# Causal attention scores accumulated across key tiles from differences of keys, in a two-layer transformer kernel

## The chip, the cores and the metric

The kernel runs on one core of one Trainium2 chip. The metric is the device time of one execution in microseconds, smaller is better. Times of before come from three runs; the profile is one more execution of the same program, recorded by the hardware profiler.

Engines in the profile: PE is TensorE's matmul, PEld its loads of stationary operands (they overlap PE), DVE is VectorE, ACT is ScalarE, POOL is GpSimd, SP issues nearly all DMAs. Matmuls write to PSUM, which has eight banks of 128 x 512 float32.

## What is computed

Two transformer layers over one sequence of S = 4096 rows of E = 256 features with 16 heads of 16. `x` is [1, 4096, 256].

```python
xn = _layernorm(x)
x = x + _L0_attn_ref(xn, ...) + _L0_ffn_ref(xn, ...)   # pass a=0: sparse attention; an fp8 product
xn = _layernorm(x)
x = x + _L1_attn_ref(xn, ...) + _L1_ffn_ref(xn, ...)   # a=1; and a block that holds a=2

# a=0: each block of 128 queries sees its own 128 keys and every 8th key, causal by an added -10000
# a=1: causal attention over all keys, queries and keys rotated (RoPE)
scores = jnp.einsum('bhqd,bhkd->bhqk', Q, K) / math.sqrt(Dh)
scores = jnp.where(causal, scores, jnp.finfo(scores.dtype).min)
attn = jax.nn.softmax(scores, axis=-1)
y = jnp.einsum('bhqk,bhkd->bhqd', attn, V)
# a=2, in _L1_ffn_ref: the same causal attention, with RMS-normalised q and k per head,
# then a mixture of four experts, two chosen for each row
```

## The kernel before

**Tiling.** Queries are worked in 8 chunks (`NCH`) of 512 (`CW`), keys in tiles of 128 (`TPC` = 4 to a chunk), heads in 4 groups (`G`) of 4 (`HPG`). A *unit* is one pass `a`, one group and one chunk of queries; there are 32 units of each pass. A causal unit of chunk `ch` (a = 1 or 2) has 4(ch + 1) key tiles, the last four of them in the queries' own chunk, where the part above the diagonal is masked. A unit of a=0 has four tiles of strided keys and one local one.

**Operands.** Each head's queries and keys are split into a rounded high part and the rest, and laid out as 64 rows a head, so that one product over 64 rows of PE gives an accurate score. `split_stored` does this for a finished half of the heads (ACT copy, POOL subtraction, two SP stores) and puts the rows into DRAM scratch `q_d` and `k_d`; `load_rows` brings them back for a unit, with tags `q`, `km` (keys for the maxima) and `ke` (keys for the exponentials). PE runs two heads at a time, one in its upper and one in its lower 64 rows: `p` in 0, 1 is the pair of heads, `j` the half. `emit` interleaves the two halves' instruction streams by their cost.

**Two passes over the keys.** First the maxima: `causal_max` multiplies a tile of 128 queries with 512 keys into two banks (`pm`), and DVE reduces each bank to one column of `mx`. Half 1's bank is reduced first, then half 0's. When all of a unit's maxima are there, `reduced`, `shift` and `shifted` turn the negated maxima into rows (`rows`, in the profile's names), in high and low parts. Then the exponentials: `causal_exp` multiplies a tile of 128 keys with the 512 queries into a bank `st`, adds the shift by a second product of a constant `pick` with `rows` (in the profile `st_a<-rows,pick_r`), adds the mask on the own chunk (`st_a<-mcol_sb,identb_sb`), and ACT writes exp(st) to `pt`. `values` multiplies the four heads' `pt` with the values (eight matmuls a key tile in the profile) and accumulates over key tiles in one bank `po`.

**PSUM.** Three rings of banks: `max` with 3 (maxima), `bank` with 4 (scores, and every other product: projections, experts), `acc` with 1 (`po`). A pair of maxima takes two banks of `max`, a pair of scores two of `bank`.

**What sets the order.** Every engine issues in the order in which the program emits (`InOrder`, line 53; so all rows of the profile show L53). The order comes from `Schedule`, a heap of pieces by a key (planned place, in units of a chunk's length) that is emptied at the end. A piece may take banks of a ring (`add_ring`), or be a *fill* that opens a bank and has a *drain* with a due time (`add_open`); `run` emits opened drains early when a ring has no room left. `unit` gives the keys: exponentials of key tile kt and pair p at a0 + 0.25 kt + 0.125 p + 0.06, values of kt 0.45 after a0 + 0.25 kt. So the order on PE in the middle of a unit is: scores of pair 0, of pair 1, values of the tile before, and so on. A unit's maxima run some units ahead (`lag`); each call of `exponentials` takes one waiting pair of maxima along as its `side`, so that a maxima product of one half runs beside a scores product of the other:

```python
own = [make(st[j], j, half_rows(j)) for j in range(2)]
emit(own[0] + side[0], side[1] + own[1])
```

The output projection of a pass and chunk (`projected`, two fills `pp` with drains `added`) comes 1.5 to 1.7 chunk lengths after the last group's unit has ended, beside the exponentials of a later unit.

**Between chunks.** For chunks 1 to 6 a section with its own place in the plan (`between`) runs the experts of chunk ch − 1, the preparation of chunk ch + 1 for a = 1 and 2 (`prepare1`: projections, rotation or norm, `split_stored`) and of chunk ch + 3 for a = 0 (`prepare0`). The first 620 us or so prepare the first chunks beside the a=0 units (`spread`).

Of the kernel before, what the change touches and what calls it, by code (L numbers as in the profile page):

```python
# [21 lines left out]
H = 16  # L22
# [43 lines left out]
class Schedule:  # L66
# [9 lines left out]
    def __init__(self):  # L76
        self.items, self.n = [], 0
        self.opened = {ring: [] for ring in self.RINGS}

    def _push(self, key, *item):  # L80
# [3 lines left out]
    def add(self, key, fn, *args):  # L84
        self._push(key, None, 0, lambda: fn(*args), None)

    def add_ring(self, key, ring, banks, fn, *args):
        self._push(key, ring, banks, lambda: fn(*args), None)

# [3 lines left out]
    def run(self):  # L93
        opened = self.opened
        while self.items or any(opened.values()):
            due, ring0 = min(((min(due for due, _ in o), r) for r, o in opened.items() if o), default=(None, None))
            if not self.items or (due is not None and due <= self.items[0][0]):
                opened[ring0].pop(0)[1]()
                continue
            _, _, (ring, banks, fn, drain) = heapq.heappop(self.items)  # L100
            if ring is not None:
                while len(opened[ring]) + banks > self.RINGS[ring]:
                    opened[ring].pop(0)[1]()
            fn()
            if drain is not None:
                opened[ring].append(drain)
# [3 lines left out]
def tile_two_layers(ctx: ExitStack, tc, d, out):  # L110
# [24 lines left out]

    def bank_tile(name, ring="bank"):
        return ps[ring].tile([P, CW], F32, tag=ring, name=name)
# [12 lines left out]
    q_d = [dram.tile([H * 4 * D, S], F32, name=f"q_d{a}") for a in range(3)]  # L150
    k_d = [dram.tile([H * 4 * D, S + (CW if a == 0 else 0)], F32, name=f"k_d{a}") for a in range(3)]
    v_d = [dram.tile([G, NCH + 1, P, TPC * VW], F32, name=f"v_d{a}") for a in range(3)]

# [9 lines left out]
    with ExitStack() as at:  # L163
# [181 lines left out]
        def split_stored(s, dst, half, col, what, name):  # L345

            hl = halves(name)
            split(s, hl)
            stored(dst, hl, half, col, what)

        def normalised(todo, x, nm, eng=None):
# [163 lines left out]
        def prepare1(ch):  # L515
# [35 lines left out]
            for n, (what, dst) in enumerate((("k", k_d[1]), ("q", q_d[1]))):  # L551
# [26 lines left out]
                for half in range(2):  # L578
# [4 lines left out]
                        ),  # L583
                    )

            act_piece(todo, weighted)
# [3 lines left out]
            for what, n, wcol, dst in (("k", 3, 1, k_d[2]), ("q", 4, 0, q_d[2])):  # L590
# [57 lines left out]
                for half in range(2):  # L648
                    act_piece(stores, lambda half=half, f=st2: f(half))
                rest.append((products, norms2, mul2, turns, stores))  # L650

# [240 lines left out]
        def load_k(u, kc, tag):  # L892
            u[tag, kc] = load_rows(u, k_d, kc * CW, tag, 3)

# [15 lines left out]
        def tt(t):  # L910
            return slice(t * P, (t + 1) * P)

        def product(dst, lhs, rhs, start=False, stop=False):

            return max(P, int(np.prod(dst.shape[1:]))), lambda: pe.matmul(dst, lhs, rhs, start=start, stop=stop)

        def own_mask(dst, eye, mask, r, blocks=0, short=0):


            got = []  # L920
            for i in (1 - short, short):
# [4 lines left out]
                if blocks:  # L926
                    m = m.unsqueeze(1).to_broadcast([64, blocks, m.shape[1]])
                got.append(product(to, eye[r, i], m, i != short and bool(blocks), i == short and not blocks))
            return got

        class Maxima:
# [10 lines left out]
            def __call__(self):  # L942
                if not self.done:
                    emit(*self.begin())
                    self.reduce()
# [110 lines left out]
        def exponentials(u, kt, p, lo, make, key):  # L1056

            mx = next_maxima(key)
            side = mx.begin() if mx else ([], [])
            st = [bank_tile(f"st_{u['nm']}_{kt}_{2 * p + j}") for j in range(2)]  # L1060
            own = [make(st[j], j, half_rows(j)) for j in range(2)]
# [8 lines left out]
        def causal_exp(u, kt, p, key):  # L1070
            kc, t = divmod(kt, TPC)
            own = kc == u["ch"]
            lo = t * P if own else 0

            def make(st, j, r):
                seq = [
                    product(st[:, lo:], u["ke", kc][p][r, tt(t)], u["q"][p][r, lo:], True),
                    product(st[:, lo:], pick[r, 0, p, :], u["sh"][r, lo:], stop=not own),
                ]
                return seq + (own_mask(st[:, lo : lo + P], identb, mcol, r) if own else [])  # L1080

            exponentials(u, kt, p, lo, make, key)
# [136 lines left out]

        sched = Schedule()  # L1220

        def put(key, fn, ring=None, drain=None, delay=0.11):
# [12 lines left out]
        def unit(a, g, ch, a0, lag, m0, own_at):  # L1235
# [21 lines left out]
            for i, make in enumerate(makes):  # L1257
                key = m0 + size * (i + 0.5) / len(makes)
                maxima.append((key, len(maxima), Maxima(make)))
                sched.add_ring(key, "max", 2, maxima[-1][2])  # L1260
            r0 = a0 - min(lag - size, 1.0)
# [5 lines left out]
            for kt in range(int(4 * size)):  # L1267
                for p in range(2):
                    key = a0 + 0.25 * kt + 0.125 * p + 0.06
                    if a:  # L1270
                        sched.add_ring(key, "bank", 2, causal_exp, u, kt, p, key)
                    elif kt < 4:
                        sched.add_ring(key, "bank", 2, strided_exp, u, kt, p, key)
                    else:
                        sched.add_ring(key, "bank", 2, local_exp, u, p, key)
                key = a0 + 0.25 * kt + 0.45
# [283 lines left out]
```

## Time and profile before

| | |
|---|---|
| three runs, median (lowest to highest) | 4963.56 us (4957.01 to 4964.4) |
| span of the profiled execution | 4961.8 us |
| its mean granted PE clock | 0.982 |
| PE, PEld busy | 4779.2 us, 2517.8 us |
| DVE, ACT, POOL busy | 3665.9 us, 3075.4 us, 886.2 us |
| products of the shift (`st_a<-rows,pick_r`) | 5248, busy 1749.6 us |
| exponentials on ACT (`pt_a<-st_a`) | 5248, busy 2590.3 us |
| plain maxima on DVE (`mx_a<-pm_a`) | 3584, busy 2220.8 us |
| DMA | 732.87 MB, queue q1 44.3% of 16 engines' span |

The profiled execution has no other time of its own than its span; the median of the runs lies 1.8 us above it. Rows of groups read "line engine op out<-in xcount | busy us, mean ns of one | idle us before them, and what ended most of it"; `64*128 64x512` is a stationary tile of 64 rows by 128 and a moving one of 64 by 512. In the timeline each row is start in us, duration in us, engine and operation; instructions of the same kind that follow closely are drawn together with their count (x4), and the bracket holds the idle time ahead of them and what ended it. In a row of windows the columns are the stretch, its length, busy us of PE, PEld, DVE, ACT and POOL with counts, the granted clock, the share of the DMA engines, and GB/s.

### The profile page before, as it was taken

Reading aid. Unit: us, or ns where it says so; the run is one execution under the profiler, and the core shown is the slowest. Engines: PE = TensorE matmul, PEld = TensorE weight load, DVE = VectorE, ACT = ScalarE, POOL = GpSimd, SP = SyncE. Lnnn points to the kernel's source line nnn. Section 1 sums busy time; section 2 is a strip of 40 time slices with the busy share of each in tenths; the row PEclk is TensorE's granted clock in tenths of the full one; section 3 lists DMA queues with packets and bytes.
Section 4 is the critical chain, followed back from the end, with each engine's and each line's share of the span. In section 5 each row is a group of like instructions: output and inputs, shape, how many; then the busy total and the mean of one; then the engine's idle time right before and its main releaser. Section 6 shows DMA issues by size and latency. Waiting matters only on the chain.

```text
span 4961.8 us, 95104 instructions
## 1 busy us (share of the span) xinstructions
PE 4779.2 (96%) x34528; PEld 2517.8 (51%) x34528; DVE 3665.9 (74%) x8399; ACT 3075.4 (62%) x6193; POOL 886.2 (18%) x1541
## 2 busy tenths in 40 slices
PE   6888899999999999999999999999999999999999
PEld 3455555555554555544545445544445544444445
DVE  4776783895689749896598984798984898989701
ACT  2555463675567547775477774677773777777752
POOL 2544423213110221103101002001002000000000
PEclk8999899999999999999999999999999999999999
DMA  6656555545544454444544334443333433333322
GB/s 205 210 157 220 188 172 167 194 152 185 175 156 138 151 191 135 147 133 153 188 129 148 129 129 129 163 135 132 125 133 110 164 131 121 124 108 128 97 81 77
DMA packets 480302, 732.87 MB, mean 148 GB/s; under 512 B 84052, under 2 KB 185940, under 8 KB 479832
## 3 DMA queue, kind: packets, MB, share of 16 engines
q1 hardware_dynamic: 477232, 725.40, 44.3%
q8 instruction: 273, 4.47, 0.4%
q10 hardware_dynamic: 2600, 1.39, 0.1%
q14 instruction: 197, 1.61, 0.1%
HBM read 582.71 MB, written 143.95 MB: 146 GB/s over the span
## 4 chain that ended last, share of the span: by engine, by line
PE 54%; DVE 6%; issue 4%; POOL 1%; ACT 0%; DMA 0%; SPq 0%; POOLq 0%; ACTq 0%; DVEq 0%
PE st_a L53 19%; PE po_a L53 16%; PE pm_a L53 8%; DVE mx_a L53 5%; PE pe_m L53 2%; PE pp L53 1%; PE pv L53 1%; PE ph_m3l L53 1%; PE ph_m2l L53 1%; PE ph_m4l L53 1%; PE ph_m5l L53 1%; PE pq L53 1%; PE ph_m7l L53 1%; PE pk L53 1%; DVE pms_a L53 0%
## 5 line engine op out<-in xcount | busy, mean ns | idle before, releaser
L53 ACT ACTIVATE pt_a<-st_a 128x512 f32<-128x512 f32 (+3 forms) x5248 | 2590.3, 574 | 1066.8 <-PE st_a L53 1003.5
L53 DVE TENSOR_REDUCE mx_a<-pm_a 128x1 f32<-128x512 f32 x3584 | 2220.8, 682 | 316.8 <-PE pm_a L53 218.8
L53 PE MATMUL pm_a<-km_a,q_a 64*128 64x512 f32 (+3 forms) x4608 | 1798.6, 434 | 50.0 <-DVE mx_a L53 45.2
L53 PE MATMUL st_a<-q_a,ke_a 64*128 64x512 f32 (+3 forms) x5632 | 1765.9, 397 | 5.4 <-ACT pt_a L53 1.8
L53 PE MATMUL st_a<-rows,pick_r 64*128 64x512 f32 (+3 forms) x5248 | 1749.6, 400 | 0.0
L53 PEld LDWEIGHTS st_a<-q_a,ke_a 64*128 64x128 f32 x5632 | 902.9, 187 | 1009.6 <-ACT pt_a L53 931.9
L53 PE MATMUL po_a<-pt_a,v 128*32 128x512 f32 (+3 forms) x11264 | 1327.4, 550 | 0.0
L53 PEld LDWEIGHTS pm_a<-km_a,q_a 64*128 64x128 f32 x4608 | 837.2, 185 | 417.3 <-DVE mx_a L53 339.7
L53 PEld LDWEIGHTS st_a<-rows,pick_r 64*128 64x128 f32 x5248 | 949.6, 186 | 56.2 <-issue 0.4
L53 DVE CUSTOM_DVE_ANT_0 pm_a<-pm_a,never_sb 128x512 f32<-128x512 f32 (+3 forms) x1024 | 477.6, 517 | 233.3 <-PE pm_a L53 195.7
L53 DVE CUSTOM_DVE_ANT_0 pms_a<-pms_a,hidden_sb 128x512 f32<-128x512 f32 x512 | 338.0, 721 | 71.2 <-PE pms_a L53 60.9
L53 PEld LDWEIGHTS po_a<-pt_a,v 128*32 128x32 f32 x11264 | 228.3, 108 | 293.8 <-issue 256.5
L53 POOL CAST pad<-nm_a 128x16 fp32r<-128x16 f32 x96 | 21.1, 219 | 1902.6 <-DVE nm_a L53 1902.6
L53 PE MATMUL pms_a<-km_a,q_a 64*128 64x512 f32 x512 | 221.7, 491 | 59.9 <-DVE mx_a L53 44.7
L53 POOL CAST rows<-tu_a 8x128 fp32r<-8x128 f32 x768 | 226.4, 295 | 214.4 <-DVE tu_a L53 119.1
L53 DVE SCALAR_TENSOR_TENSOR acc_m<-pe_m,g_wt_m,acc_m 128x192 f32<-128x192 f32 x128 | 53.2, 417 | 246.3 <-PE pe_m L53 243.1
L53 PE MATMUL st_a<-mcol_sb,identb_sb 64*128 64x128 bf16 (+1 forms) x2048 | 233.2, 209 | 0.0
L53 DVE DVE_READ_ACCUMULATOR2_ANT mx_a<- 128x1 f32 x1536 | 216.9, 141 | 0.0
L53 POOL TENSOR_TENSOR om_a<-od_a,rd_a 128x256 f32<-128x256 f32 x96 | 64.6, 673 | 675.7 <-DVE rd_a L53 651.8
L53 PEld LDWEIGHTS pms_a<-km_a,q_a 64*128 64x128 f32 x512 | 96.7, 192 | 99.8 <-DVE mx_a L53 80.1
L53 PEld LDWEIGHTS <-identb_sb 64*128 64x128 bf16 x2048 | 114.6, 96 | 9.1 <-issue 1.5
L53 POOL TENSOR_TENSOR xa<-xa,pa 128x512 f32<-128x512 f32 (+1 forms) x48 | 56.9, 1184 | 237.3 <-issue 118.8
(406 smaller groups left out, 3942.2 us busy)
## 6 DMA issues: line engine op xcount, KB each, us to landing
km_a<-k_d SPq DMA_DIRECT2D x352, 512.0 KB, 4.8
ke_a<-k_d SPq DMA_DIRECT2D x352, 512.0 KB, 3.9
k_d<-hl_k SPq DMA_DIRECT2D x100, 512.0 KB, 3.9
q_d<-hl_q SPq DMA_DIRECT2D x96, 512.0 KB, 4.7
q_a<-q_d SPq DMA_DIRECT2D x96, 512.0 KB, 5.1
v<-v_d SPq DMA_DIRECT2D x352, 136.0 KB, 4.8
w_l<-in_l_dram SPq DMA_DIRECT2D x80, 256.0 KB, 2.9
w<-in_w_dram SPq DMA_DIRECT2D x69, 256.0 KB, 5.0
```

The lines of the kernel that those rows point to most:

```text
L53: got = emit(*args, **kw)
```

## The change

For the causal passes the four score banks of a unit are now taken once, at its first key tile, and kept to its last. The first key tile writes keys times queries and adds the shift. Every later key tile adds the product of the queries with the *difference* of its 128 keys to the 128 keys of the tile before, so that the bank holds the new tile's shifted scores. The mask of an own-chunk tile stays in the columns that later tiles no longer touch.

The differences are made where keys are prepared: `steps_stored` runs after each store of keys of a = 1 and 2 (two halves, eight chunks: 32 calls). It subtracts on POOL the 128 columns before from each 128 columns, fetches the last 128 columns of the chunk before from a DRAM scratch `last_d` by SP (28 calls) and leaves its own there (28 calls), and splits and stores the result like keys into `e_d` (ACT copy, POOL subtraction, two SP stores of 512 KB). `ke` of the causal passes is loaded from `e_d`, of the same size; `km` still from `k_d`.

`Schedule` keeps a count of held banks. While a unit holds its four, `free_ring` sends other fills of ring `bank` to ring `max`. `add_ring` is gone; pieces reserve their banks themselves when they run. Units of a=0 keep their own banks and shift for each tile.

```diff
--- before.py
+++ after.py
@@ -76,6 +76,19 @@
     def __init__(self):
         self.items, self.n = [], 0
         self.opened = {ring: [] for ring in self.RINGS}
+        self.held = 0
+
+    def reserve(self, ring, banks):
+        held = self.held if ring == "bank" else 0
+        while len(self.opened[ring]) + held + banks > self.RINGS[ring]:
+            self.opened[ring].pop(0)[1]()
+
+    def hold(self, banks):
+        self.held += banks
+
+    def free_ring(self, ring="bank"):
+
+        return "max" if ring == "bank" and self.held else ring
 
     def _push(self, key, *item):
         heapq.heappush(self.items, (key, self.n, item))
@@ -83,9 +96,6 @@
 
     def add(self, key, fn, *args):
         self._push(key, None, 0, lambda: fn(*args), None)
-
-    def add_ring(self, key, ring, banks, fn, *args):
-        self._push(key, ring, banks, lambda: fn(*args), None)
 
     def add_open(self, key, ring, fill, due, drain):
         self._push(key, ring, 1, fill, (due, drain))
@@ -99,8 +109,8 @@
                 continue
             _, _, (ring, banks, fn, drain) = heapq.heappop(self.items)
             if ring is not None:
-                while len(opened[ring]) + banks > self.RINGS[ring]:
-                    opened[ring].pop(0)[1]()
+                ring = self.free_ring(ring)
+                self.reserve(ring, banks)
             fn()
             if drain is not None:
                 opened[ring].append(drain)
@@ -133,7 +143,10 @@
         for kind, n in rings.items():
             ps[kind] = stack.enter_context(tc.tile_pool(name=f"ps_{kind}{stage}", bufs=n, space=PSUM))
 
-    def bank_tile(name, ring="bank"):
+    sched = Schedule()
+
+    def bank_tile(name, ring=None):
+        ring = ring or sched.free_ring()
         return ps[ring].tile([P, CW], F32, tag=ring, name=name)
 
     def load(name, shape, dtype=F32, pool=const, src=None, eng=None):
@@ -149,6 +162,8 @@
 
     q_d = [dram.tile([H * 4 * D, S], F32, name=f"q_d{a}") for a in range(3)]
     k_d = [dram.tile([H * 4 * D, S + (CW if a == 0 else 0)], F32, name=f"k_d{a}") for a in range(3)]
+    e_d = [None] + [dram.tile([H * 4 * D, S], F32, name=f"e_d{a}") for a in (1, 2)]
+    last_d = dram.tile([2, 2, P, P], F32, name="last_d")
     v_d = [dram.tile([G, NCH + 1, P, TPC * VW], F32, name=f"v_d{a}") for a in range(3)]
 
 
@@ -347,6 +362,21 @@
             hl = halves(name)
             split(s, hl)
             stored(dst, hl, half, col, what)
+
+        def steps_stored(k, a, ch, half, name):
+
+            s = work.tile([P, CW], F32, tag="r1", name=f"step_{name}", bufs=2)
+            last = last_d[a - 1, half]
+            if ch:
+                sp.dma_start(s[:, :P], last)
+            if ch + 1 < NCH:
+                sp.dma_start(last, k[:, CW - P :])
+            pool.tensor_tensor(s[:, P:], k[:, P:], k[:, : CW - P], ALU.subtract)
+            if ch:
+                pool.tensor_tensor(s[:, :P], k[:, :P], s[:, :P], ALU.subtract)
+            else:
+                pool.tensor_copy(s[:, :P], k[:, :P])
+            split_stored(s, e_d[a], half, ch * CW, "k", f"e{name}")
 
         def normalised(todo, x, nm, eng=None):
 
@@ -582,6 +612,11 @@
                             parts[half][0], dst, half, ch * CW, what, f"{what}1{half}{nm}"
                         ),
                     )
+                    if what == "k":
+                        act_piece(
+                            todo,
+                            lambda half=half, parts=parts: steps_stored(parts[half][0], 1, ch, half, f"1{half}{nm}"),
+                        )
 
             act_piece(todo, weighted)
             v_products(todo, lambda: s["xt"], lambda: w[2], 1, ch, None, nm)
@@ -647,6 +682,10 @@
                 turn(turns, lambda z=z: z["raw"], ev2, f"pt{name}{nm}")
                 for half in range(2):
                     act_piece(stores, lambda half=half, f=st2: f(half))
+                    if what == "k":
+                        act_piece(
+                            stores, lambda half=half, z=z: steps_stored(z[half, 0], 2, ch, half, f"2{half}{nm}")
+                        )
                 rest.append((products, norms2, mul2, turns, stores))
 
             (pk, nk, mk, tk, sk), (pq, nq, mq, tq, sq_) = rest
@@ -890,7 +929,7 @@
             u["mx"] = work.tile([P, TPC, HPG, NCH], F32, tag="mx", name="mx_" + u["nm"], bufs=4)
 
         def load_k(u, kc, tag):
-            u[tag, kc] = load_rows(u, k_d, kc * CW, tag, 3)
+            u[tag, kc] = load_rows(u, e_d if u["a"] and tag == "ke" else k_d, kc * CW, tag, 3)
 
         vbufs, v_no = [], [0]
         for i in range(5):
@@ -910,11 +949,13 @@
         def tt(t):
             return slice(t * P, (t + 1) * P)
 
-        def product(dst, lhs, rhs, start=False, stop=False):
-
-            return max(P, int(np.prod(dst.shape[1:]))), lambda: pe.matmul(dst, lhs, rhs, start=start, stop=stop)
-
-        def own_mask(dst, eye, mask, r, blocks=0, short=0):
+        def product(dst, lhs, rhs, start=False, stop=False, partial=False):
+
+            return max(P, int(np.prod(dst.shape[1:]))), lambda: pe.matmul(
+                dst, lhs, rhs, start=start, stop=stop, skip_group_check=partial
+            )
+
+        def own_mask(dst, eye, mask, r, blocks=0, short=0, partial=False):
 
 
             got = []
@@ -925,7 +966,7 @@
                     m, to = m[:, part], dst[:, :, part] if blocks else dst[:, part]
                 if blocks:
                     m = m.unsqueeze(1).to_broadcast([64, blocks, m.shape[1]])
-                got.append(product(to, eye[r, i], m, i != short and bool(blocks), i == short and not blocks))
+                got.append(product(to, eye[r, i], m, i != short and bool(blocks), i == short and not blocks and not partial, partial))
             return got
 
         class Maxima:
@@ -941,6 +982,7 @@
 
             def __call__(self):
                 if not self.done:
+                    sched.reserve("max", 2)
                     emit(*self.begin())
                     self.reduce()
 
@@ -1056,8 +1098,20 @@
         def exponentials(u, kt, p, lo, make, key):
 
             mx = next_maxima(key)
+            if mx:
+                sched.reserve("max", 2)
             side = mx.begin() if mx else ([], [])
-            st = [bank_tile(f"st_{u['nm']}_{kt}_{2 * p + j}") for j in range(2)]
+            if not u["a"]:
+                sched.reserve("bank", 2)
+                st = [bank_tile(f"st_{u['nm']}_{kt}_{2 * p + j}", "bank") for j in range(2)]
+            elif kt == 0:
+                sched.reserve("bank", 2)
+                sched.hold(2)
+                st = u["st", p] = [bank_tile(f"st_{u['nm']}_{2 * p + j}", "bank") for j in range(2)]
+            else:
+                st = u["st", p]
+            if u["a"] and kt == TPC * (u["ch"] + 1) - 1:
+                sched.hold(-2)
             own = [make(st[j], j, half_rows(j)) for j in range(2)]
             emit(own[0] + side[0], side[1] + own[1])
             for j in range(2):
@@ -1073,11 +1127,10 @@
             lo = t * P if own else 0
 
             def make(st, j, r):
-                seq = [
-                    product(st[:, lo:], u["ke", kc][p][r, tt(t)], u["q"][p][r, lo:], True),
-                    product(st[:, lo:], pick[r, 0, p, :], u["sh"][r, lo:], stop=not own),
-                ]
-                return seq + (own_mask(st[:, lo : lo + P], identb, mcol, r) if own else [])
+                seq = [product(st[:, lo:], u["ke", kc][p][r, tt(t)], u["q"][p][r, lo:], kt == 0, partial=True)]
+                if kt == 0:
+                    seq.append(product(st[:, lo:], pick[r, 0, p, :], u["sh"][r, lo:], partial=True))
+                return seq + (own_mask(st[:, lo : lo + P], identb, mcol, r, partial=True) if own else [])
 
             exponentials(u, kt, p, lo, make, key)
 
@@ -1216,8 +1269,6 @@
                 pool.tensor_tensor(sums, sums, x, ALU.add)
                 sp.dma_start(xs_d[ch, :, two, :], sums)
 
-
-        sched = Schedule()
 
         def put(key, fn, ring=None, drain=None, delay=0.11):
             if drain is None:
@@ -1257,7 +1308,7 @@
             for i, make in enumerate(makes):
                 key = m0 + size * (i + 0.5) / len(makes)
                 maxima.append((key, len(maxima), Maxima(make)))
-                sched.add_ring(key, "max", 2, maxima[-1][2])
+                sched.add(key, maxima[-1][2])
             r0 = a0 - min(lag - size, 1.0)
             sched.add(r0 - 0.04, reduced, u, len(keys))
             at_, step = (0.21, 0.06) if lag - size > 0.9 else (-0.03, 0.03)
@@ -1268,11 +1319,11 @@
                 for p in range(2):
                     key = a0 + 0.25 * kt + 0.125 * p + 0.06
                     if a:
-                        sched.add_ring(key, "bank", 2, causal_exp, u, kt, p, key)
+                        sched.add(key, causal_exp, u, kt, p, key)
                     elif kt < 4:
-                        sched.add_ring(key, "bank", 2, strided_exp, u, kt, p, key)
+                        sched.add(key, strided_exp, u, kt, p, key)
                     else:
-                        sched.add_ring(key, "bank", 2, local_exp, u, p, key)
+                        sched.add(key, local_exp, u, p, key)
                 key = a0 + 0.25 * kt + 0.45
                 if a:
                     kc, t = divmod(kt, TPC)
```

## Prediction

> **What bounds the kernel now.** I read the page first, then a window of the late chunks, then the timeline of one key tile, since an average share cannot say what ends each period.
>
> ```profile
> span 4961.8 us, 95104 instructions
> PE 4779.2 (96%) x34528; PEld 2517.8 (51%) x34528; DVE 3665.9 (74%) x8399; ACT 3075.4 (62%) x6193; POOL 886.2 (18%) x1541
> L53 ACT ACTIVATE pt_a<-st_a 128x512 f32<-128x512 f32 (+3 forms) x5248 | 2590.3, 574 | 1066.8 <-PE st_a L53 1003.5
> L53 DVE TENSOR_REDUCE mx_a<-pm_a 128x1 f32<-128x512 f32 x3584 | 2220.8, 682 | 316.8 <-PE pm_a L53 218.8
> L53 PE MATMUL st_a<-rows,pick_r 64*128 64x512 f32 (+3 forms) x5248 | 1749.6, 400 | 0.0
> L53 PEld LDWEIGHTS pm_a<-km_a,q_a 64*128 64x128 f32 x4608 | 837.2, 185 | 417.3 <-DVE mx_a L53 339.7
> ```
>
> PE looks like the bound (96%) and the shift product `st_a<-rows` looks dear (1749.6 us). The last row disturbs that: PE's weight loads for the maxima waited 339.7 us for DVE's reductions. In the late chunks, where most causal work lies, DVE is nearly as full as PE:
>
> ```profile
> 3968.00:4588.00 620.00, 619.00 (x4816) 288.96 (x4816) 558.93 (x1065) 457.97 (x923) 30.38 (x83) 1.00 0.37 122
> ```
>
> The columns after the length are busy us of PE, PEld, DVE, ACT and POOL, then the granted clock. DVE is 558.93/620 = 90% busy, ACT 74%. One key tile of that stretch follows: start, duration, engine, work.
>
> ```profile
> 4222.42 0.49 PE L53 MATMUL pm_a<-km_a,q_a 64*128 64x512 f32 x1
> 4222.99 2.48 DVE L53 TENSOR_REDUCE mx_a<-pm_a 128x1 f32<-128x512 f32 x4 [0.26 <-PE st_a L53]
> 4223.25 2.07 ACT L53 ACTIVATE pt_a<-st_a 128x512 f32<-128x512 f32 x4 [0.67 <-PE st_a L53]
> 4223.45 0.39 PE L53 MATMUL st_a<-rows,pick_r 64*128 64x512 f32 x1
> 4223.73 0.18 PEld L53 LDWEIGHTS pm_a<-km_a,q_a 64*128 64x128 f32 x1 [0.32 <-DVE mx_a L53]
> 4223.74 0.50 PE L53 MATMUL pm_a<-km_a,q_a 64*128 64x512 f32 x1
> 4223.74 0.50 PE L53 MATMUL st_a<-rows,pick_r 64*128 64x512 f32 x1
> 4224.17 1.06 PE L53 MATMUL po_a<-pt_a,v 128*32 128x512 f32 x8
> 4225.16 0.49 PE L53 MATMUL st_a<-q_a,ke_a 64*128 64x512 f32 x1
> ```
>
> The period is 4225.16 − 4222.42 = 2.74 us. The maxima have three PSUM banks and come two at a time, so the second pair's last product (4223.74) needs the bank that the first pair filled first. Its reduction starts at 4222.99 and lasts 2.48/4 = 0.62, to 4223.61; PE answers 0.13 later. The values start 0.43 after that, take 0.99 to the next key tile, whose first maximum reaches DVE 0.57 later (4225.73 by the same offsets: 4222.99 − 4222.42). The closed loop is 0.62 + 0.13 + 0.43 + 0.99 + 0.57 = 2.74, the whole period. No shift product stands in it: the last one starts at 4223.74 together with the waiting maximum, in the other half of PE's rows.
>
> **What the change does, part by part.**
>
> *Shift products removed.* There are 2 x 4 x 8 = 64 causal units, with 8 x 4 x 36 = 1152 key tiles of four shift products, 4608; 256 stay. Products of the two row halves start in pairs 0.23 us apart (4223.22, 4223.45 in this timeline), so a key tile has two slots, 0.46 us, less for PE. In the loop above PE then comes to the same maximum 0.46 us earlier and waits for the same reduction: worth nothing in the 735 key tiles that I count with a period of 2.70 to 2.77. What covers it is DVE's chain; were it gone, each would gain up to 0.26 (DVE's idle part of the period), the first rival.
>
> It pays where PE is not waiting for DVE. (1) The own chunk's four key tiles carry eight mask products a tile and have periods 2.94, 2.60, 2.31 and 1.85 from 4002.18 on. There the waiting product starts 0.16 after DVE's release allows in the first tile, 0.08 in the second, none and 0.05 in the last two: 0.29 a unit, 56 units (the first chunk's eight are counted below): −16. Bounds: 0, and all slots, narrowing with the tile, 0.46 + 0.36 + 0.24 + 0.16 = 1.22 x 56 = −68. I take the low value as the rows give the release times themselves. (2) The last unit has no maxima beside it; two key tiles take 4.6 us (2.48 and 2.14), of which ACT is busy 4.19; half of the 0.41 idle, over 15 pairs, gives −4 (bounds 0 and −6). (3) Key tiles beside first-layer maxima and the first chunk's own tiles: −8, from their shift slots that no DVE wait follows (0 to −16).
>
> *Banks pinned.* The four score banks no longer rotate, but two pairs of two in a ring of four came back in the same order anyway: before, `ke` of a pair already waited for the exponentials of the same pair one key tile ago, and it does so in the shadow of the values. Exponentials now begin one slot earlier and end earlier; 0, between −2 and +5.
>
> The Trainium skill's page Perfetto Trace Analysis, section Optimizing Tensor Performance, asks that independent products rotate through PSUM banks so that ACT and DVE empty one while the next is filled, which speaks against pinning; if that rule held here, and each of the 1152 key tiles showed one exponential of 574 ns, the sum would be +681 instead of +20 (an estimate). No run before shows a pinned bank.
>
> *Other bank users.* While a causal unit holds four banks, fills go to the maxima's ring. In steady state these are the output projections `pp`: 24 (pass, chunk) times two = 48.
>
> ```profile
> 3672.55 1.99 PE L53 MATMUL pp<-wp_sb,ot_a 128*128 128x256 f32 x8
> 3674.48 0.50 PE L53 MATMUL st_a<-q_a,ke_a 64*128 64x512 f32 x1
> 3675.04 2.48 DVE L53 TENSOR_REDUCE mx_a<-pm_a 128x1 f32<-128x512 f32 x4 [1.83 <-PE pm_a L53]
> 3675.95 0.18 PEld L53 LDWEIGHTS st_a<-q_a,ke_a 64*128 64x128 f32 x1 [0.48 <-ACT pt_a L53]
> 3676.27 0.59 ACT L53 COPY pa<-pp 128x512 f32<-128x512 f32 x1
> 3676.60 1.06 PE L53 MATMUL po_a<-pt_a,v 128*32 128x512 f32 x8
> ```
>
> Before, the key tile after a `pp` takes 3676.60 − 3674.48 = 2.12 to its values, with a wait for an exponential since `pp` took one score bank. After, `pp` leaves two banks to the maxima. The second pair's first product then waits for one reduction (0.56 + 0.62 + 0.13 = 1.31), its second for the next (1.93), and the values follow 0.43 later at 2.36: +0.24, times 48 = +12. Bounds: 0, and a whole reduction each, 0.62 x 48 = +30.
>
> *The steps of the keys.* 32 calls of `steps_stored`, 28 with a load. Each adds, queued in order: an SP load of 64 KB and an SP write, POOL subtractions of 3/4 and 1/4 of a 128x512 tile (by the hl row's 1.27 us: 0.95 and 0.32), an ACT copy of 0.62, a POOL subtraction of 1.27, and two SP stores of 512 KB. As work that is POOL 2.54 x 32 = 81 us of an engine 82% idle, ACT 20, DMA 34 MB on 733; DMA is at 0.58 share in the fullest between-chunk window I read and stays below that limit, so 0 for those. As a wait: ACT's copy stands in ACT's queue behind the loaded columns, and these behind SP's stores of the keys, which need POOL's last subtraction: 1.27 + 2.2 (the shortest landings of 256 KB stores are 2.0 and 2.2; bounds 2.0 and 2.9) + 0.32 = 3.8, less the 0.62 copy beside it: 3.2 for a pair of calls. Behind that copy stand the evacuations of PE's next fills. In the six sections between chunks PE is the bound:
>
> ```profile
> 2356.00:2480.00 124.00, 123.39 (x607) 71.86 (x605) 66.17 (x146) 61.99 (x116) 23.35 (x24) 1.00 0.58 190
> ```
>
> so a stall of ACT that reaches PE counts. Four sections that also prepare the first layer lose 3.2 in the rotary pass, two lose 2, and the last pass, with more slack, 0.5 in each of six: 12.8 + 4 + 3 = +20. Bounds: 0 (ACT, half idle there, catches up) and 12 pairs x 3.2 = +38. The eight early calls lie in the first 620 us, where PE waits anyway (101 of 124 busy in its last fifth): +10 (0 to +26, all at 3.2), and the fills there that now go to the maxima's ring +6 (0 to +12).
>
> **The sum.** −16 − 4 − 8 + 12 + 20 + 10 + 6 = +20 on the profiled execution's span of 4961.8, so 4982. The median of the runs is 4963.56, 1.8 above that span; the forecast is 4961.8 + 20 + 1.8 = 4983.6, say 4984. All gains at their ends and no cost give 4963.6 − 92 = 4872, all costs and no gain 4963.6 + 111 = 5075; ends will not all meet, and half of each gives 4918 and 5019.
>
> **Rivals.** *PE is the bound and the removal pays.* For it: PE 96%, and PE's own cadence in the loop leaves hardly 0.05 us more of waiting than two slots explain. Against it: the closed loop without shift. If the loop can be pulled in, DVE's 2.48 binds: 0.26 x 735 = −191, less the sum's other terms, about 4785. Chance 0.06.
>
> *Gains without costs.* The mechanism is slack: if ACT's copies wait on PE's fills longer than 3.2 us ahead (ACT is 62.0 of 124 us busy there), the steps and early calls are hidden, and the own-chunk gain stays: −28 + 12 = −16, or about −50 if the own chunk also gains half of its slots. This ends faster, 4910 to 4950. It decides once the stall costs under half of what I took. Chance 0.16.
>
> *Nothing to see.* Gains and costs cancel within 0.2%, 10 us, about the least that a measurement of this kernel can tell: 0.2.
>
> *A lowered clock.* PE would now idle in many short waits. In the window 496 to 620 PE is busy 101 of 124 and its clock 0.82; after the change the loop would leave PE busy about (2.74 − 0.46)/2.74 = 0.83, the same share. If the clock followed to 0.82, the loop's PE parts (0.43 + 0.99 + 0.57 = 1.99) would grow by 0.44, times 735 = +320, near 5300. Against it: the early idle comes in waits up to 13 us, the new ones are under 0.8. Decides when the granted clock of the late windows leaves 1.00. Chance 0.04; a part of it, in a tenth of the run, is 5015 to 5050, chance 0.08. The page TensorE: Matmul & The Clock Gate, section A second HAM failure mode: psum-queue depth-cycling, warns of just such short idling between groups that cycle through PSUM; by that rule the sum would be this rival's, and the late window above, with its short waits at a clock of 1.00, does not show it.
>
> *The forecast's case*, +10 to +55: 0.46.
>
> Range: 4925 to 5040, leaving out 0.06 + 0.04 and a part of the neighbours. Faster 0.22, same 0.20, slower 0.58; the likeliest case alone: 4974 to 5019.
>
> **What would show it.** Right: the period in a late window stays 2.73 to 2.75 while `st_a<-rows` falls to 896 products (640 first-layer, 256 causal) and PE's share to 83 to 90%; the wait PEld pm_a <- DVE mx_a grows from 339.7 by about 0.46 x 735 = 338, to some 680; key tiles after `pp` take 0.2 longer; sections between chunks are 2 to 5 us longer, with ACT waiting for POOL's step. Wrong: a period near 2.5, sections of equal length, or a clock below 1.00 late.

## The result, and the profile after

The changed kernel takes 5105.59 us (median of four, 5100.98 to 5113.79) against 4963.98 for the kernel before on the same chip: a ratio of 1.029, with a 95% interval of 1.0276 to 1.0305. It is 142 us slower. The forecast was 4984, with a range to 5040.

First the page of the kernel after: span, the busy row, three groups (busy, mean ns | idle before, and what ended it).

```profile
span 5112.0 us, 83557 instructions
...
PE 4526.5 (89%) x30176; PEld 2178.0 (43%) x30176; DVE 3678.4 (72%) x8399; ACT 3090.9 (60%) x6225; POOL 969.7 (19%) x1637
...
L53 PEld LDWEIGHTS pm_a<-km_a,q_a 64*128 64x128 f32 x4608 | 786.4, 187 | 800.3 <-DVE mx_a L53 750.8
...
L53 PE MATMUL st_a<-rows,pick_r 64*128 64x512 f32 x896 | 317.3, 429 | 0.0
...
L53 ACT CAST hl_e<-step 128x512 fp32r<-128x512 f32 x32 | 19.8, 618 | 241.9 <-POOL step L53 241.9
```

PE is busy 253 us less, and the span has grown by 150. The shift is down to 896 products and is busy 317.3 us, 1432 less than before; PE's weight loads for the maxima wait for DVE 750.8 us where it was 339.7. So PE's freed time became waiting. The last row is new: ACT's 32 copies of the differences are 19.8 us of work, ahead of which ACT stood 241.9 us for POOL.

A key tile in the late part, timeline of the kernel after:

```profile
4402.67 0.50 PE L53 MATMUL st_a<-q_a,ke_a 64*128 64x512 f32 x1
4402.67 0.73 PE L53 MATMUL pm_a<-km_a,q_a 64*128 64x512 f32 x2
...
4403.24 2.48 DVE L53 TENSOR_REDUCE mx_a<-pm_a 128x1 f32<-128x512 f32 x4 [0.26 <-PE pm_a L53]
...
4403.98 0.50 PE L53 MATMUL pm_a<-km_a,q_a 64*128 64x512 f32 x1 [0.35 <-DVE mx_a L53]
...
4404.41 1.07 PE L53 MATMUL po_a<-pt_a,v 128*32 128x512 f32 x8
...
4405.41 0.50 PE L53 MATMUL st_a<-q_a,ke_a 64*128 64x512 f32 x1
```

The period is 4405.41 − 4402.67 = 2.74 us, as before, without a shift product in sight. PE now stands 0.35 us at the maximum that needs the bank, and DVE still has its 0.26 of idle. Counted from values to values, 737 key tiles had a period of 2.70 to 2.77 before, and 735 after. So the loop did what was said. The granted clock (the third column from the end) stayed 1.00 in this stretch:

```profile
4352.00:4480.00 128.00, 113.26 (x798) 42.11 (x798) 117.06 (x214) 96.41 (x192) 3.33 (x11) 1.00 0.34 118
```

Where the time went is seen by setting the 96 units of both traces side by side, by the copy of each unit's output: the first 21 units (the first 620 us) end 33 us later, the six stretches with a section between chunks are 119 us longer together (17 to 23 each), the last unit is 6 shorter, all other units together are unchanged within 0.2, and what follows the last unit's copy is 5 longer. In one such section (rows of ACT, of POOL, of SP's queue and of PE, kernel after):

```profile
2433.35 0.62 ACT L53 CAST hl_e<-step 128x512 fp32r<-128x512 f32 x1 [7.59 <-POOL step L53]
2433.87 0.58 ACT L53 COPY xt<-pt 128x512 f32<-128x512 f32 x1
2434.35 0.62 ACT L53 CAST hl_k<-r_k 128x512 fp32r<-128x512 f32 x1
2434.87 0.59 ACT L53 COPY xt<-pt 128x512 f32<-128x512 f32 x1
2444.01 0.62 ACT L53 CAST hl_e<-step 128x512 fp32r<-128x512 f32 x1 [8.55 <-POOL step L53]
```

```profile
2443.52 0.45 POOL L53 TENSOR_TENSOR step<-r_k,step 128x128 f32<-128x128 f32 x1 [5.57 <-DMA step<-last_d]
```

```profile
2433.99 1.87 SPq L53 DMA_DIRECT2D e_d<-hl_e  x2
2435.95 1.59 SPq L53 DMA_DIRECT2D k_d<-hl_k  x2
2437.63 1.15 SPq L53 DMA_DIRECT2D w_e3a<-in_e3a_dram  x1
2438.88 1.19 SPq L53 DMA_DIRECT2D w_e0d<-in_e0d_dram  x1
2440.12 0.57 SPq L53 DMA_DIRECT2D step<-last_d  x1
```

```profile
2434.50 2.59 PE L53 MATMUL pk<-xt,w 128*128 128x512 f32 x4 [3.28 <-ACT xt L53]
...
2545.28 0.79 PE L53 MATMUL st_a<-q_a,ke_a 64*128 64x512 f32 x1 [6.55 <-ACT y L53]
```

ACT's copy of the second half's keys starts at 2434.35, the copy of its differences at 2444.01. Between them ACT does one more copy and then stands 8.55 us: the copy at the head of its queue waits for POOL, POOL waits for the fetched columns, and SP issues the fetch only at 2440.12, behind the differences' stores of the first half, the keys' stores of the second and two weight loads. Behind ACT's copy stand the evacuations `xt`, `y` and `n_q`, and PE waits for them, 3.28 and 6.55 us. In this section (2399 to 2607) the four copies waited 31.5 us, and the section grew by 19. In all 28 calls with a fetch POOL stood waiting for it, 137.9 us in all.

The second of PE's waits has a price of its own. The stretch after it, in windows of the kernel after and of the same place before (length, busy PE, PEld, DVE, ACT, POOL, then the granted clock):

```profile
2531.00:2553.00 22.00, 14.59 (x79) 9.97 (x78) 6.24 (x21) 10.51 (x20) 10.39 (x10) 0.77 0.75 270
```

```profile
2416.00:2438.00 22.00, 21.39 (x106) 15.88 (x105) 8.50 (x23) 9.96 (x17) 9.18 (x8) 1.00 0.55 175
```

A product of 64 by 512 takes 0.79 us at 2545.28, where the late loop shows 0.50. Over the six sections the clock is 0.93 to 0.95, where it was 0.99. The kernel without the differences (the first experiment) issues the same number of PE products there; it takes 1081.7 us for the six, with PE busy 1025.5, and the kernel after takes 1198.5, with PE busy 1062.4. So of the 117 us between them some 80 are PE standing still and some 37, by this estimate, the lowered clock.

### The profile page after: what moved, and what is told of

Read it like the earlier page. It is cut to its first block, busy times and chain, and to the rows that moved or that the text cites. A ratio compares the mean times of both kernels' runs of the same rounds, so it can differ in the third digit from the quotient of the medians.

```text
span 5112.0 us, 83557 instructions
## 1 busy us (share of the span) xinstructions
PE 4526.5 (89%) x30176; PEld 2178.0 (43%) x30176; DVE 3678.4 (72%) x8399; ACT 3090.9 (60%) x6225; POOL 969.7 (19%) x1637
## 4 chain that ended last, share of the span: by engine, by line
PE 55%; DVE 26%; issue 8%; POOL 5%; DMA 3%; ACT 2%; SPq 0%; ACTq 0%; POOLq 0%; DVEq 0%
PE po_a L53 19%; DVE mx_a L53 18%; PE st_a L53 11%; PE pm_a L53 9%; DVE pms_a L53 3%; DVE pm_a L53 3%; PE pv L53 2%; PE pk L53 2%; PE pp L53 2%; PE pq L53 1%; POOL x L53 1%; PE pe_m L53 1%; PE pms_a L53 1%; PE ph_m7l L53 1%; DVE od_a L53 1%
## 5 line engine op out<-in xcount | busy, mean ns | idle before, releaser
L53 PE MATMUL pm_a<-km_a,q_a 64*128 64x512 f32 (+3 forms) x4608 | 1695.2, 441 | 341.3 <-DVE mx_a L53 324.2
L53 PE MATMUL st_a<-q_a,ke_a 64*128 64x512 f32 (+3 forms) x5632 | 1856.7, 416 | 73.7 <-ACT y L53 28.2
L53 PEld LDWEIGHTS pm_a<-km_a,q_a 64*128 64x128 f32 x4608 | 786.4, 187 | 800.3 <-DVE mx_a L53 750.8
L53 PE MATMUL st_a<-rows,pick_r 64*128 64x512 f32 x896 | 317.3, 429 | 0.0
L53 PE MATMUL st_a<-mcol_sb,identb_sb 64*128 64x64 bf16 (+1 forms) x2048 | 246.6, 212 | 0.0
L53 PEld LDWEIGHTS st_a<-rows,pick_r 64*128 64x128 f32 x896 | 168.8, 195 | 7.3 <-issue 0.4
L53 ACT CAST hl_e<-step 128x512 fp32r<-128x512 f32 x32 | 19.8, 618 | 241.9 <-POOL step L53 241.9
```

What stands on the lines that cost most here:

```text
L53: got = emit(*args, **kw)
```

## The experiments

Three theories were set against each other. "Wait": ACT's copy of the differences, in line before it is ready. "Work": the added stores, copies and DMA themselves. "Banks": pinned banks, fills in the maxima's ring, a lowered clock. Beside them "loop" against "PE" on what sets the key tile's period. Each ratio is to runs of the kernel before made beside that kernel (medians 4961.19 to 4963.84).

**Without the differences.**

```diff
 def steps_stored(k, a, ch, half, name):
+    return
 ...
-u[tag, kc] = load_rows(u, e_d if u["a"] and tag == "ke" else k_d, kc * CW, tag, 3)
+u[tag, kc] = load_rows(u, k_d, kc * CW, tag, 3)
 ...
-act.activation(pt[:, lo:], st[j][:, lo:], AF.Exp)
+act.activation(pt[:, lo:], st[j][:, lo:], AF.Exp, scale=1e-4)
```

> The changed kernel without the differences: nothing is subtracted, split, stored or loaded for them, and the later key tiles add the products with the plain keys (so the banks hold other sums; the exponential takes a scale of 1e-4 to stay finite). Pinned banks, the fills in the maxima's ring and the single shift stay. Theory 'wait' (the loss of 142 us is ACT's copy of the differences, which stands first in ACT's queue until POOL and the fetched columns are ready, 242 us in all): the loss goes with it, about 4955 us, 4940 to 4975, with sections between chunks as long as before. Theory 'work' (the loss is the extra stores, DMA and engine work of the differences): the same here. Theory 'banks' (the loss comes from pinned banks, from fills that take a bank of the maxima, or from a clock lowered by PE's idling in the loop): above 5050.

Measured: 4952.81, ratio 0.9979 (0.997 to 0.9989). "Banks" is out as the cause of the loss: all of it, 153 us against the changed kernel, goes with the differences, and the sections are 2 us longer than before in all.

**The same stores, without waiting for POOL.**

```diff
-s = work.tile(...); last = ...; (fetch, leave, subtractions)
-split_stored(s, e_d[a], half, ch * CW, "k", f"e{name}")
+split_stored(k, e_d[a], half, ch * CW, "k", f"e{name}")
```

> The changed kernel, but the differences' split and stores take the keys themselves: no fetched columns, no subtraction of the tile before; the ACT copies, POOL's split and the 64 stores of 512 KB stay and read what is ready anyway (the sums are others; exponential scaled by 1e-4). Theory 'wait': 4955 to 4985, at most 25 above the kernel without the differences. Theory 'work': 5060 or more, close to the 5106 of the changed kernel. Theory 'banks': above 5050.

Measured: 4999.46, ratio 1.0077 (1.0062 to 1.0092). That is 47 above the kernel without differences, nearly twice what "wait" allowed, and 106 below the change. The trace points to a wait of another kind. The splits go through two pairs of buffers, and four splits in a row now outrun the stores; in the waits of this kernel (us in all, times, longest):

```profile
ACT hl_k L53 <- DMA k_d<-hl_k: 50.8, 12, 8.0
...
ACT hl_e L53 <- DMA e_d<-hl_e: 20.0, 10, 3.9
```

The kernel before has no wait of ACT's `hl_k` for a store at all; only `hl_q` waits for one there, 5.7 us. That these waits make up the 47 us was not shown by a run of its own.

**A sum that restarts at each chunk.**

```diff
-if ch:
-    sp.dma_start(s[:, :P], last)
-if ch + 1 < NCH:
-    sp.dma_start(last, k[:, CW - P :])
 pool.tensor_tensor(s[:, P:], k[:, P:], k[:, : CW - P], ALU.subtract)
-if ch: pool.tensor_tensor(s[:, :P], k[:, :P], s[:, :P], ALU.subtract)
-else: pool.tensor_copy(s[:, :P], k[:, :P])
+pool.tensor_copy(s[:, :P], k[:, :P])
 ...
-product(st[:, lo:], u["ke", kc][p][r, tt(t)], u["q"][p][r, lo:], kt == 0, partial=True)
+product(st[:, lo:], u["ke", kc][p][r, tt(t)], u["q"][p][r, lo:], t == 0, partial=True)
-if kt == 0:
+if t == 0:
```

> The running sum starts anew at each chunk of 512 keys: the first key tile of a chunk uses plain keys and adds the shift again (1152 shift products instead of 256), so no columns of the chunk before are fetched or left. Still queued behind ACT's copy of the keys: POOL's split of them (1.27), POOL's subtraction (1.0) and a copy of 128 columns before the ACT copy of the differences. Theory 'wait': ACT's wait for a call falls from 7.6 to some 3.3 us, and the loss over the kernel without the differences to 3.3/7.6 of it: about 5015, 4980 to 5040. Theory 'work': 5080 or more. Theory 'banks': 5080 or more.

Measured: 5013.13, ratio 1.0103 (1.0088 to 1.0118). In the trace ACT's wait for POOL's step fell from 241.9 us to

```profile
ACT hl_e L53 <- POOL step L53: 98.5, 30, 5.9
```

which is 3.3 us a wait, and the sections are now 5 to 9 us longer than before, not 17 to 23. The fetch with its place in the queues cost 92 us of the 142, although 896 shift products come back here.

**The shift once, nothing else** (the kernel before).

```diff
-    product(st[:, lo:], ke, q, True),
-    product(st[:, lo:], pick[r, 0, p, :], u["sh"][r, lo:], stop=not own),
+    product(st[:, lo:], ke, q, True, stop=kt > 0 and not own)]
+if kt == 0:
+    seq.append(product(st[:, lo:], pick[r, 0, p, :], u["sh"][r, lo:], stop=not own))
```

> The kernel before, with rotating banks and plain keys, without the shift products of all causal key tiles but a unit's first (4352 left out; exponential scaled by 1e-4). Theory 'loop' (the key tile's period of 2.74 us is closed through three maxima banks, a reduction and the values; no shift product in it): period 2.74 as before, gains only on own chunks and in the last unit, 4920 to 4955. Rival 'PE' (PE's throughput sets the period): period near 2.5, about 4785, at most 4850.

Measured: 4932.44, ratio 0.9938 (0.9923 to 0.9953). Leaving 4352 products out for nothing brings 30 us. The period is 2.74 in 739 key tiles. "Loop" stands, "PE" falls. Between this kernel and the one without the differences lie pinned banks and the fills in the maxima's ring: 20 us by the medians, 35 by the two profiled executions, of which 9 in the first 21 units, 1 in the sections, 22 in the other units and the rest behind the last one. Of these 22, 21 lie in the units with `pp`: the five that hold two pairs are 1.5 to 1.6 us shorter than before with rotating banks, and 0.8 to 1.1 longer with pinned ones.

**ACT's copy moved.** The fetch, the scratch and the subtractions stay where the change has them; POOL's split and the stores go with the copy. The value products move too: in pass a = 1 ahead of the queries' projection, in a = 2 behind the keys' stores.

```diff
 steps_stored(...)            # as in the change, but returns s
 ...
 act_piece(todo, weighted)
 v_products(...)
+for half in range(2):
+    split_stored(step[half], e_d[a], half, ch * CW, "k", ...)   # ACT copy, POOL split, stores
```

> The changed kernel with its fetched columns, its scratch and its POOL subtractions where they were; only the ACT copy of the differences, with the POOL split and the stores behind it, is moved behind the value products of the preparation. If it is ACT's queue that costs (evacuations of PE's fills behind a copy that waits for POOL and the fetch): some 120 of the 142 us come back, 4975 to 5005. If the fetch costs by itself (POOL's queue stands for it and SP's queue for POOL, whatever ACT does): 5050 or more.

Measured: 4980.56, ratio 1.0032 (1.002 to 1.0043). 125 of the 142 us come back. POOL still stands for the fetch, 102.8 us in 28 waits (137.9 in the change), and the kernel hardly feels it. PE's waits for ACT, 3.6 us in all in the kernel before and 98.8 in the change, are 16.0 here. So it was ACT's queue, and not the fetch by itself. How much of the 125 comes from the moved value products, which the edit takes along, no run shows; the next one gives a hint.

**The differences in place, split late, with the restart.**

```diff
+def steps(k):
+    for i in reversed(range(1, TPC)):
+        now = k[:, i * P : (i + 1) * P]
+        pool.tensor_tensor(now, now, k[:, (i - 1) * P : i * P], ALU.subtract)
 ...
+# split_stored(k, e_d[a], ...) of both halves behind v_products
```

> As the sum restarted at each chunk, but the differences are made in place by three POOL subtractions of 128 columns behind the keys' own split, and their ACT copy, POOL split and stores come later, behind both halves' keys and the value products, so that ACT's copy finds them ready and the two pairs of buffers of a split have been stored. Theory 'wait': ACT's waits for POOL and for the stores go, and the time comes to that without the differences, 4953, plus up to 15: 4950 to 4975. Rival 'work' (the extra copies, splits and stores themselves cost the 47 us that the kernel storing the keys twice showed over the one without): 4990 to 5010.

Measured: 4974.69, ratio 1.0029 (1.0017 to 1.0041), 22 above the kernel without the differences: at the upper edge of "wait", well below "work". Some 20 us remain for 32 more splits; which queue they are lost in was not taken apart. The value products stand here as in the run before. The first 21 units end at 613.8 us, against 620.6 in the kernel without the differences, which does less work there; so the moved order seems to gain some 7 us early by itself, and the splits may cost as much more than the 22. For the sections that was not measured.

**One running sum over the unit, waits mended.**

```diff
+sp.dma_start(last_d[a - 1, ch, half], k[:, CW - P :])        # before the keys' split
+sp.dma_start(last, last_d[a - 1, ch - 1, half])              # behind the keys' stores
+pool.tensor_tensor(k[:, :P], k[:, :P], last, ALU.subtract)   # right before the late split
```

> The full change, one running sum over all key tiles of a unit, with its waits mended: the chunk's last columns are left before the split, the ones of the chunk before are fetched behind the keys' stores and subtracted only right before the late split. Theory 'wait' with 'loop': as the sum restarted at each chunk with the late split (4975), since a shift more or less is worth nothing in the loop of 2.74: 4960 to 4990. Rival (each fetch costs a wait wherever it stands): 5010 or more.

Measured: 4971.67, ratio 1.0019 (1.001 to 1.0029). The whole change, with its waits mended (ACT's copies of the differences still stand 24.9 us for POOL, in 17 waits, instead of 241.9 in 32), costs 8 us. It gains nothing, since the loop does not care for the shift.

**The values in two halves.** From a unit's second key tile on:

```diff
-sched.add(key, values, u, kt, ...)
+for part in range(lo // (CW // 2), 2):
+    sched.add(key - 0.08 * (1 - part), half_values, u, kt, kc, t, lo, part, ...)
```

`half_values` multiplies 256 of the 512 queries; the first half lands between the two pairs of scores. On the restarted sum:

> The sum restarted at each chunk, and from a unit's second key tile on the values of a key tile are two sets of products, of 256 queries each, one behind each pair of scores, instead of one set of 512 behind both. Theory 'loop' (the period of 2.74 is the chain third maxima bank, reduction, second pair, values, next pair): with half the values between two pairs the chain falls to some 2.25, DVE's four reductions of 0.62 bind instead, and the period falls to 2.5 to 2.6: 0.15 to 0.24 x 700 key tiles, from 5013 to about 4870, 4835 to 4920. Rival 'PE': PE then pays 0.2 more for the second turn from half to full rows in each period without gaining: 5013 or above, to 5150.

Measured: 4916.7, ratio 0.991 (0.9895 to 0.9925): 96 us faster than the same without the halves, at the upper end of what was expected. On the kernel before:

> The kernel before, shift products and all, with the values split in the same way. By the theory 'loop' together with PE's own cadence of 2.69 in this kernel: PE becomes the bound at 2.69 + 0.2, so +0.15 x 735: about 5075, 5030 to 5120. If PE had room left in the kernel before (the loop alone were the bound): about 4964 - 150, 4800 to 4850.

Measured: 5135.51, ratio 1.0354 (1.0338 to 1.0369), slower by 174, more than the 156 expected at most: the most frequent period is 2.93 us instead of the 2.89 expected, and PE is busy 500.0 us of the 500 from 4200 on. The same edit gains where PE has room and loses where it has none. With the late split:

> Both edits: the differences' split moved behind the value products of the preparation, and the values in two halves. If the theories 'wait' and 'loop' both hold, the gains add: 4960 - 143 = about 4815, 4770 to 4880, below the kernel before. If one falls: 4870 to 4960, or above 5000.

Measured: 4878.41, ratio 0.9832 (0.9815 to 0.9848), at the upper edge. The timeline shows the new loop, and why the gain stayed under its bound:

```profile
4301.31 8.67 DVE L53 TENSOR_REDUCE mx_a<-pm_a 128x1 f32<-128x512 f32 x14 [0.18 <-PE pm_a L53]
...
4306.89 0.49 PE L53 MATMUL st_a<-q_a,ke_a 64*128 64x512 f32 x1
...
4307.55 0.64 PE L53 MATMUL po_a<-pt_a,v 128*32 128x256 f32 x8
...
4308.12 0.49 PE L53 MATMUL st_a<-q_a,ke_a 64*128 64x512 f32 x1
...
4309.59 0.50 PE L53 MATMUL st_a<-q_a,ke_a 64*128 64x512 f32 x1
```

DVE reduces 14 banks with no gap, 0.62 each; half a key tile takes 4308.12 − 4306.89 = 1.23, a whole one 2.46. On the first key tile of a chunk, where the shift comes back, half a tile takes 4309.59 − 4308.12 = 1.47. So the restart, free in the loop of 2.74, has a price here, and the running sum without it was tried:

> The same with the values in two halves from a unit's second key tile on. With the restart, the split period was 2.46 but 2.94 on each chunk's first key tile, where the shift came back; 8 x 28 = 224 such tiles now lose the shift: -0.46 x 224 = -103 from 4878, so 4775, 4755 to 4810. If DVE binds on those tiles as well, less: 4810 to 4850.

Measured: 4800.3, ratio 0.9665 (0.965 to 0.9679), computing all that the reference does, and 164 us faster than the kernel before. It is 78 us below the restarted sum, where 103 were expected, within the range. That is the best version here: it needs the change, with its waits mended, and the split values that let the loop use the time the change frees.

## Why the prediction was wrong

*The loop* (the shift in it worth nothing) was right: period 2.74 in 735 key tiles, PE's wait for DVE at 750.8 us where some 680 were forecast, PE's share 89% within 83 to 90, late clock 1.00. The kernel with the shift once settles it.

*The small gains* were forecast at −28 for own chunks, mixed tiles and the last unit. The kernel with the shift once shows −30 in its time, but that agreement is partly luck. Unit by unit its profiled execution (39 us shorter) has −9 in the first 21 units, −6 in the last, −9 in the units without `pp`, about 0.2 for a causal unit where 0.29 was forecast, and −13 in the units with `pp`, for which the forecast had no gain. The −4 of the last unit was a slip besides: half of 0.41 over 15 pairs is −3. In the change itself, gains and `pp` cancel in the units between, within 0.2.

*Pinned banks and `pp`*: forecast 0 and +12 and, early, +6, 18 in all; the kernels with the shift once and without the differences put them at 20 to 35 together.

*The steps of the keys* is the term that failed. Forecast +20 in six sections (2 to 5 us each), at most +38, and +10 in the first 620 us; measured +119 in the sections and some +33 in the first 21 units, all terms there together. The mechanism was named, ACT's copy at the head of its queue with the evacuations of PE's fills behind it, but its size came from a wrong count: 3.2 us for a *pair* of calls, from 1.27 for POOL, 2.2 for a landing, 0.32 and less 0.62. The trace has 7.6 for *each* call (241.9/32), and some 8.4 for each of the 24 in the sections. Three things are in the difference. The two halves do not overlap: the second fetch is issued behind the first half's stores and two weight loads, 5 us after ACT's copy of the keys has ended (2440.12 against 2434.97). The fetch of 64 KB lands after 3.3 us (median), not 2.2: that figure was taken from stores of 256 KB, while loads of 256 KB took 2.8 to 5.6 us in the kernel before. And POOL is not free at once: it begins the split of the keys 1.4 us after ACT's copy of them, on average, and its last subtraction takes 0.45, not 0.32. Over the 28 calls with a fetch, 4.9 us pass from the end of ACT's copy of the keys to the issue of the fetch, 3.9 from there to POOL's last subtraction, and 0.5 to ACT's copy of the differences, in the mean. The bound of +38 multiplied the same 3.2 by pairs, though the early bound of +26 took it for each call; the prediction's own chain of 3.8 for each call would have given 24 x 3.8 = 91 in the sections and 8 x 3.8 = 30 early. The "more slack" of the last pass (0.5 a section) was wrong too: it is behind its second call that PE waits 6.55 us in the section shown, and 6.1 to 7.7 in each of the six.

The sum put the clock at nothing. The rival of a lowered clock looked for it in the late loop, where it stayed 1.00; it came in the sections, with PE's long waits, and by the estimate above made some 37 us of their loss.

The four splits in a row through two pairs of buffers were not in the sum either (the kernel that stores the keys twice is 47 us slower than the one without the differences): of a step that is added, its buffers' next users count too.

## What to carry to other kernels

Before an instruction is taken off a busy engine, close the loop of one period in the timeline and see if it stands in it; a busy share of 96% did not say so, and leaving the work out altogether brought 0.6%. What the removal freed was worth something only together with an edit that broke the loop: the values in halves cost 3.5% alone and brought 3.4% on top of the mended change. An operation that depends on a fetch should not stand in an engine's queue directly behind what starts the fetch: moving one copy, with its split and stores, behind work that was there anyway returned 125 of 142 us.

## What the runs showed of the hardware

One wait of 6.55 us of PE came with a granted clock of 0.77 in the 22 us around its end, with products of 64 by 512 at 0.79 us; the late loop, with PE standing 0.35 us in each 2.74, kept a clock of 1.00 and 0.50. The Trainium skill's page TensorE: Matmul & The Clock Gate, section HAM oscillation — how this bites in real kernels, says to avoid gaps of PE longer than about 3.4 us; these two cases agree with it. A wait a little shorter is no safe one here: the 3.28 us that ended at 2434.50 were followed by a clock of 0.51 from 2436.0 to 2439.4. The warning of the same page, section A second HAM failure mode: psum-queue depth-cycling, of short idling between groups that cycle through PSUM, weighed in the prediction, is not borne out by this loop.

Eight products of 32 columns over 256 queries take 0.64 us, and over 512 queries 1.06 to 1.07. The next product starts 0.57 after the shorter set (4307.55 to 4308.12) and 1.00 after the longer (4404.41 to 4405.41), so two halves take some 0.14 more than one whole: little while PE has room, and dear where it has none, as the values in halves on the kernel before show.
